# Two layers of graph attention on one core: a second-last superchunk's sums in three parts, and indices doubled step by step

## The chip, the cores and the metric

The kernel runs on one core of a Trainium2 chip. Its five engines work side by side, each through its own queue of instructions in order: PE (TensorE, matrix products), DVE (VectorE), ACT (ScalarE), POOL (GpSimd) and SP (SyncE, which here only issues transfers). They wait for each other through semaphores. The metric is the device time of one execution in microseconds; the lower, the better. Every kernel is run several times, and the median is told.

## The reference

A layer norm and a relu, then two layers of graph attention (GAT) over 6250 nodes with 256 features and 200,000 edges that are sorted by their destination, then a residual. Cut to what matters:

```python
def _add_self_loops(src, dst, ea, n):
    cnt = segment_sum(ones, dst)
    loop = segment_sum(ea, dst) / maximum(cnt, 1.0)[:, None]
    return concat([src, idx]), concat([dst, idx]), concat([ea, loop])

def _gat(x, src, dst, ea, Wg, a_s, a_d, Wge, a_e, b, n, h, f):
    hx = (x @ Wg).reshape(n, h, f)
    he = (ea @ Wge).reshape(-1, h, f)
    al = leaky_relu(einsum(hx, a_s)[src] + einsum(hx, a_d)[dst] + einsum(he, a_e), 0.2)
    al = exp(al - segment_max(al, dst)[dst])
    al = al / segment_sum(al, dst)[dst]
    return segment_sum(hx[src] * al[:, :, None], dst).reshape(n, h * f) + b

h = maximum(layernorm(x), 0.0)
te = relu(edge_attr @ We0 + be0) * exp(h @ Wo0 + bo0)[src][:, None]
h1 = relu(_gat(h, *_add_self_loops(src, dst, te), 4 heads of 64) + h)
te = relu(edge_attr @ We1 + be1) * exp(h1 @ Wo1 + bo1)[src][:, None]
h2 = _gat(h1, *_add_self_loops(src, dst, te), 1 head of 256) + h1
out = x + h2 + h
```

So each edge fetches the transformed row of its source, scales it by a softmax weight over the edges of the same destination, and the rows are added up by destination. Layer 1 needs all rows that layer 0 has made.

## The kernel before

**Steps.** The 200,000 edges are 1563 chunks of 128. Chunks are grouped into 66 superchunks a layer: 64 of 24 chunks, then one of 14 and one of 13. One step handles one superchunk of one layer; 132 steps in all, each with a dictionary (`st` for the step at hand, `nx` for the next, `pv` for the one before, `late` for the one before that, `after` for the first step of the next layer). In a superchunk each of the 128 partitions holds a run of C neighbouring edges.

**What a step does.** `gather(st)` issues one indirect DMA for each chunk from POOL's queue; it fetches 128 rows of a table in HBM (`self.T[l]`, seen as `self.rows[l]`) into the tile G, by the indices in `self.src[:, o:o+C]`, and between two of them POOL writes a small tile, `gap` (L799, L803). There are three buffers of G. The rows of layer 1's table are twice as long as those that are gathered, so its indices are the sources times two; L750 doubles them, all 1563 columns in one DVE instruction, while layer 0 ends.

`logits` (DVE) computes the attention logits and two scans along the partition's edges, which give maxima by destination within the partition. `ends` has PE transpose the scans' last columns into the PSUM tile `lf`; `links` (DVE) scans these across partitions, from the state that the superchunk before left, and has PE transpose the result back. `maxima` (DVE, ACT) ends with the exponentials in `k_w`. `scale` (DVE) multiplies the gathered rows by them, `carried` (DVE) adds in row 0 what the superchunk before leaves for a destination that both have. `onehots` builds S, a matrix for each chunk that says which edge belongs to which destination, and `sums` (PE) adds up the products S x G of all chunks in one PSUM tile, u. `evict` (ACT) copies it to the SBUF tile U.

`spread`, `parts`, `blocks`, `rphase1`, `rphase2`, `adst` and `edge_rows` prepare for the next step what depends on the edge attributes and on the destinations (`rphase1` yields in the middle, and uses PE and ACT).

**Finish and rows.** `finish` is `nodes0` or `nodes1`. Both begin with `merge`, small DVE instructions and an ACT exponential that join the self loop to the sums; in layer 0 follow an ACT relu `hw` (marked by `st["hw"]`) and six elementwise instructions of 256 columns, which an argument can put on POOL instead of DVE; in layer 1 two DVE instructions make the output rows `o`. In layer 0, `rows1` transposes the new rows on PE with a copy on ACT, `rows2` multiplies them by the next layer's weights into the PSUM tile `fin` (there is one), and `rows3` adds the bias (DVE, L434), takes an exponential (ACT) and writes the rows to `self.T[1]` by a DMA of SP's queue. In layer 1 `rows1` and `rows2` do nothing and `rows3` writes `o` to the output: by SP's queue for the first 64 superchunks, and for the last two by an indirect DMA of POOL's queue, whose index tile two DVE instructions make at that place (L1247, L1248). Writes to the same tensor at addresses known only at run time wait for each other.

**The last two superchunks of a layer** are handled together by `ending`, once for layer 0 (then `after` is layer 1's first step) and once for layer 1 (then `after` is None). In it `st` is the superchunk of 14 chunks, `nx` that of 13. The order of the calls is the order in every engine's queue: nothing is scheduled anew. After layer 0, `gather(after)` can start only when all of `self.T[1]` has been written. `ending` gives `finish` of `pv` and of `st` to POOL (`Z`). `sums(nx, first=1)` starts with chunk 1 and takes chunk 0, which `carried` changes, last.

Of the kernel before, what the change touches and what calls it, by code (L numbers as in the profile page):

```python
# [22 lines left out]
F32 = mybir.dt.float32  # L23
BF = mybir.dt.bfloat16
I32 = mybir.dt.int32
AF = mybir.ActivationFunctionType
OP = mybir.AluOpType
# [4 lines left out]
P = 128  # L32
C = 24
# [46 lines left out]
class Kernel:  # L80
# [480 lines left out]
    def index_group(self, g, pool, di):  # L561
# [23 lines left out]
        for pen, e in zip((self.fpen, self.lpen), ends):  # L585
            t = pool.tile([P, 4 * C], F32, name="gt", bufs=2)
            e3 = e.to_broadcast([P, n, c])
            V.tensor_sub(v3(t[:, :w]), *((d3, e3) if pen is self.fpen else (e3, d3)))
            yield
            V.tensor_scalar(pen[:, o:o + w], t[:, :w], 1.0, -BIG, op0=OP.min, op1=OP.mult)  # L590
            yield
# [117 lines left out]
    def ending(self, st, nx, pv, late, after):  # L709

        nc, k = self.nc, st["k"]
        Z = nc.gpsimd
        self.load_lb(k + 3)
        self.gather(nx)
        drain(self.logits(st))
        self.ends(st)
        self.spread(nx)
        self.parts(nx)
        y = self.rphase1(nx)
        next(y)  # L720
        self.links(st)
        if late:
            self.rows2(late)
        self.blocks(nx)
        drain(y)
        self.load_ea(k + 2)
        self.rphase2(nx)
        self.adst(nx)
        drain(self.maxima(st))
        drain(self.scale(st))  # L730
        self.carried(st)
        self.sums(st)
        self.edge_rows(nx)
        drain(self.logits(nx))
        self.ends(nx)
        self.onehots(nx)
        if late:
            self.rows3(late)
        if pv:
            drain(self.finish(pv, Z))  # L740
        self.links(nx)
        self.load_fl(k + 2)
        drain(self.maxima(nx))
        self.evict(st)
        y = self.rphase1(after) if after else iter(())
        next(y, None)
        c = nx["C"]
        drain(self.scale(nx, cuts=(1, 1 + c // 2, c)))
        if after:
            nc.vector.tensor_scalar(self.src, self.src, 2.0, None, op0=OP.mult)  # L750
        drain(self.scale(nx, cuts=(0, 1)))
        self.carried(nx)
        self.sums(nx, first=1)
        self.evict(nx)
        drain(self.finish(st, Z))
        if pv:
            self.rows1(pv)
            self.rows2(pv)
            self.rows3(pv)
        drain(y)  # L760
        f = self.finish(nx)
        while after and "hw" not in nx:
            next(f)
        self.rows1(st)
        self.rows2(st)
        drain(f)
        self.rows3(st)
        self.rows1(nx)
        self.rows2(nx)
        self.rows3(nx)  # L770
        if after:
            self.gather(after)
            self.nodes(after)
            self.spread(after)
            self.parts(after)
            self.blocks(after)
            self.rphase2(after)
            self.adst(after)
            self.edge_rows(after)
            self.onehots(after)  # L780
# [224 lines left out]

    def ends(self, st):


        e = st["ends"]
        self.nc.tensor.transpose(self.lf[0:e.shape[1], 1:P + 1], e, self.ident)  # L1010
# [85 lines left out]
                                    .to_broadcast([P, c1 - c0, H, L.F]), op=OP.mult)  # L1096
            yield

    def sums(self, st, first=0):
        nc, L, c = self.nc, st["L"], st["C"]  # L1100
        G, S = st["G"], st["S"]
        st["u"] = self.ps_1.tile([P, 512], F32, name="u")
        for j in range(c):
            i = (j + first) % c
            nc.tensor.matmul(st["u"][:, :L.W], S[:, i, :], G[:, i, 0:L.W], start=(j == 0), stop=(j == c - 1))  # L1105

    def evict(self, st):
        L = st["L"]
# [125 lines left out]
    def rows3(self, st):  # L1234
        nc, L, s = self.nc, st["L"], st["s"]
        if L.l == 0:
            self.table_row(st)
            r = self.row(0, s)
            nc.sync.dma_start(self.T[1][ds(r, M), :], st["trow"][1:M + 1, :])
            return  # L1240
        o, out = st["o"], self.a["out"]
        if s < self.direct:
            r = self.row(1, s)
            nc.sync.dma_start(out[ds(r, M), :], o[1:M + 1, :])
        else:
            idx = self.np_.tile([P, 1], I32, name="oidx")
            nc.vector.tensor_add(idx, self.base_f[:, s:s + 1], self.iota_m)  # L1247
            nc.vector.memset(idx[0:1, :], 1 << 20)  # L1248
            nc.gpsimd.indirect_dma_start(  # L1249
                out=out[:, :], out_offset=bass.IndirectOffsetOnAxis(ap=idx[:, 0:1], axis=0), in_=o,  # L1250
                in_offset=None, bounds_check=self.N - 1, oob_is_err=False)
# [119 lines left out]
def drain(g):  # L1371
    for _ in g:
        pass
# [93 lines left out]
```

## Time and profile before

| | us |
|---|---|
| median of 3 runs | 4556.36 |
| lowest and highest of them | 4551.79, 4559.2 |
| the profiled execution | 4555.93 |
| its span, from the first instruction to the last | 4554.1 |
| POOL busy | 3915.8 (86%) |
| PE busy | 3065.9 (67%) |
| DVE busy | 2901.8 (64%) |
| ACT busy | 516.8 (11%) |

The profile comes from one execution. Its page gives busy time by engine and groups of instructions; a row of a group has the line, engine, operation, output and inputs, the count, the busy time, the mean of one in ns, the idle time of the engine before them, and which other work ended that idle time. Rows in order of time have the start and the duration in us, then the instruction, and in brackets the engine's idle time before it and what ended it. Where a row says "issue", the engine waited for nothing that the profile shows. Several like instructions in a row can be merged (x2, x28). PEld are PE's weight loads. fp32 products go through PE in two passes, so the sums of 14 chunks show as x28.

### The profile page before, as it was taken

The numbers are of one execution on the slowest core, as the hardware profiler recorded it, in microseconds if no ns is written. First come the engines' busy times: TensorE is split into PE (matmuls) and PEld (weight loads), VectorE is DVE, ScalarE is ACT, GpSimd is POOL, SyncE is SP. The second block draws the span as 40 slices with busy tenths as digits, with TensorE's granted clock in tenths as the row PEclk, the third lists the DMA queues.
The fourth block names the chain that finished last, engine by engine and source line by source line (L and its number), as shares of the span: only waits on it lengthen the run. The fifth ranks groups of instructions, "written<-read, shape, count | busy, mean of one in ns | idle before, by whom it ended". The sixth has DMA issues, their size and how long they took to land. (4 is left out here: it accounts for less than half of the span.)

```text
span 4554.1 us, 37613 instructions
## 1 busy us (share of the span) xinstructions
PE 3065.9 (67%) x9916; PEld 1899.5 (42%) x9916; DVE 2901.8 (64%) x6675; ACT 516.8 (11%) x1150; POOL 3915.8 (86%) x6365
## 2 busy tenths in 40 slices
PE   8777677667677677677746566666666665666665
PEld 6444444444444344444424334333343343433433
DVE  7877667677677677676745555555554555555655
ACT  5111111111111111111100000000000000000000
POOL 6888888888888888888878888888888888888885
PEclk9877777777777777777767777777777777777777
DMA  6444444444444444444434444444444444444442
GB/s 224 130 136 134 126 129 136 124 127 136 125 128 135 125 128 135 125 130 134 119 98 124 116 128 122 118 128 128 111 128 121 124 123 128 122 116 122 128 116 74
DMA packets 231112, 576.39 MB, mean 127 GB/s; under 512 B 63097, under 2 KB 87871, under 8 KB 230825
## 3 DMA queue, kind: packets, MB, share of 16 engines
q0 software_dynamic: 150144, 422.75, 35.2%
q1 hardware_dynamic: 80331, 150.52, 10.0%
q8 instruction: 79, 1.29, 0.1%
q14 instruction: 142, 1.16, 0.1%
q10 hardware_dynamic: 416, 0.67, 0.1%
HBM read 542.72 MB, written 31.09 MB: 126 GB/s over the span
## 5 line engine op out<-in xcount | busy, mean ns | idle before, releaser
L799 POOL DMA_INDIRECT G<-T,src x3102 | 2969.6, 957 | 553.1 <-issue 518.7
L1105 PE MATMUL u<-G,S 128*128 128x270 f32 (+1 forms) x6252 | 1461.0, 393 | 106.7 <-DVE G L1085 97.6
L1105 PEld LDWEIGHTS u<-G,S 128*128 128x128 f32 x6252 | 1189.5, 192 | 388.0 <-DVE G L1085 162.1
L803 POOL MEMSET gap<- 128x208 f32 x3102 | 893.3, 288 | 1.8
L1095 DVE TENSOR_TENSOR G<-G,kps 128x6144 f32<-128x6144 f32 (+3 forms) x136 | 853.0, 6274 | 0.0
L885 PE MATMUL y<-ea,webd 64*128 64x384 f32 (+1 forms) x1056 | 749.7, 860 | 67.3 <-ACT R L890 66.7
L1010 PE MATMUL lf<-ident,fb 128*36 128x128 f32 (+1 forms) x132 | 53.3, 404 | 1093.3 <-DVE fb L1002 772.3
L987 DVE TENSOR_TENSOR G<-rt,G 128x96 f32<-128x96 f32 (+1 forms) x132 | 30.2, 228 | 1138.9 <-DMA G<-T,src 1138.6
L1010 PEld LDWEIGHTS lf<-ident,fb 128*36 128x36 f32 (+1 forms) x132 | 15.7, 119 | 1134.6 <-DVE fb L1002 819.2
L899 PE MATMUL zad<-R,wea 128*64 128x384 f32 (+1 forms) x1056 | 476.0, 815 | 0.5 <-DVE aq L952 0.3
L890 ACT ACTIVATE R<-y,webd 128x768 f32<-128x768 f32 x260 | 233.2, 897 | 2015.2 <-PE lf L1027 1647.7
L930 DVE TENSOR_TENSOR S<-kps,loc 128x3072 f32<-128x3072 f32 x132 | 437.5, 3315 | 4.5
L885 PEld LDWEIGHTS y<-ea,webd 64*128 64x128 f32 x1056 | 300.9, 314 | 311.8 <-issue 192.5
L899 PEld LDWEIGHTS zad<-R,wea 128*64 128x64 f32 x1056 | 160.7, 207 | 319.0 <-issue 214.0
L945 PE MATMUL zad<-a,Q 128*128 128x12 bf16 (+1 forms) x132 | 24.9, 188 | 174.6 <-DVE a L943 174.6
L430 PE MATMUL fin<-wg,h1T 128*128 128x260 f32 x264 | 135.3, 667 | 2.3 <-ACT h1T L1200 2.3
L973 DVE STREAM_TRANSPOSE rt<-zad 128x768 f32<-128x768 f32 (+1 forms) x130 | 124.9, 960 | 12.1 <-PE zad L959 11.2
L914 DVE TENSOR_TENSOR lb<-lb,kps 128x1536 bf16<-128x1536 bf16 (+1 forms) x68 | 112.7, 1658 | 0.0
L1110 ACT ACTIVATE U<-u 128x270 f32<-128x270 f32 (+1 forms) x132 | 51.9, 393 | 493.7 <-PE u L1105 493.7
L1041 DVE SCALAR_TENSOR_TENSOR m<-fpen,lf,m 128x24 f32<-128x24 bf16 (+1 forms) x66 | 16.4, 249 | 132.8 <-PE lf L1027 132.6
L945 PEld LDWEIGHTS <-Q 128*128 128x128 bf16 x132 | 13.7, 104 | 208.3 <-DVE a L943 198.6
L430 PEld LDWEIGHTS fin<-wg,h1T 128*128 128x128 f32 x264 | 75.6, 316 | 52.1 <-issue 36.6
(201 smaller groups left out, 2287.5 us busy)
## 6 DMA issues: line engine op xcount, KB each, us to landing
G<-T,src POOLq DMA_INDIRECT x3102, 2.8
ea<-in_ea_dram SPq DMA_DIRECT2D x64, 768.0 KB
lb<-locrow SPq DMA_DIRECT2D x64, 384.0 KB
T<-t1row SPq DMA_DIRECT2D x66, 227.5 KB
tw<-T SPq DMA_DIRECT2D x66, 225.8 KB
tw<-T SPq DMA_DIRECT2D x66, 117.2 KB
tw<-in_x_dram SPq DMA_DIRECT2D x66, 112.0 KB
out_dram<-fb SPq DMA_DIRECT2D x64, 112.0 KB
```

The lines of the kernel that those rows point to most:

```text
L430: self.nc.tensor.matmul(ps[:, :L.MW], hT[:, k, :], self.wg[L.l][:, k, :], start=(k == 0), stop=(k == 1))
L799: nc.gpsimd.indirect_dma_start(out=G[:, c, 0:L.TW], out_offset=None, in_=self.rows[L.l][0:n * (1 + L.l), :], in_offset=bass.IndirectOffset ...
L803: nc.gpsimd.memset(self.gap, 0.0)
L885: nc.tensor.matmul(y[:, o], self.webd[l][r, :], ea[r, w], start=True, stop=True)
L890: nc.scalar.activation(R[:, i, :32 * c].rearrange("p (b n) -> p b n", b=2), y.rearrange("p (b n) -> p b n", b=2)[:, :, :16 * c], AF.Relu, ...
L899: nc.tensor.matmul(st["zad"][i * PH:(i + 1) * PH, o], self.wea[l][0], R[:, i, w], start=True, stop=False)
L914: V.tensor_tensor(lb[:, :, :n], lb[:, :, :n], self.k_part.unsqueeze(2).to_broadcast([P, i, n]), op=OP.is_equal)
L930: nc.vector.tensor_tensor(st["S"][:, c0:c1, :], self.k_iota.unsqueeze(1).to_broadcast(w), self.loc[:, o + c0:o + c1].unsqueeze(2).to_broad ...
L973: V.transpose(rv[:, :32 * c].rearrange("p (b n) -> p b n", b=2), z.rearrange("p (b n) -> p b n", b=2)[:, :, :16 * c])
L1010: self.nc.tensor.transpose(self.lf[0:e.shape[1], 1:P + 1], e, self.ident)
L1095: nc.vector.tensor_tensor(v, v, pw[:, c0:c1, :].unsqueeze(3) .to_broadcast([P, c1 - c0, H, L.F]), op=OP.mult)
L1105: nc.tensor.matmul(st["u"][:, :L.W], S[:, i, :], G[:, i, 0:L.W], start=(j == 0), stop=(j == c - 1))
```

## The change

In `ending`, the sums of `st` are no longer issued in one piece. `sums` takes ranges of chunks and can be called several times for one step: the first third, then the logits and `ends` of `nx`, the second third, then the one-hots and links of `nx`, and the last third. `sums(nx, (1, c), (0, 1))` is the order of before (chunk 0 last). The finish of `pv` and its place before the links, and the row of `late`, move behind the sums of `nx`; finish never uses POOL any more. The finish of `st` comes before the eviction of `nx`, wholly in layer 1, and up to its `hw` in layer 0. In layer 1 the rows of `pv` and `st` are written as soon as their finish is issued; in layer 0 the row of `pv` follows the finish of `st`, and the row of `st` stands inside the finish of `nx`, behind its `hw`.

The index tiles of the two indirect writes are made at the start of `ending`. And `src` is doubled in `ends` of each step of layer 0, for that step's columns, behind the logits that have waited for their gather; the doubling of all columns is gone.

```diff
     def ending(self, st, nx, pv, late, after):
         nc, k = self.nc, st["k"]
-        Z = nc.gpsimd
         self.load_lb(k + 3)
         self.gather(nx)
+        for q in () if after else (st, nx):
+            q["idx"] = idx = self.np_.tile([P, 1], I32, name="oidx")
+            nc.vector.tensor_add(idx, self.base_f[:, q["s"]:q["s"] + 1], self.iota_m)
+            nc.vector.memset(idx[0:1, :], 1 << 20)
         drain(self.logits(st))
         self.ends(st)
...
         self.carried(st)
-        self.sums(st)
+        c, h = nx["C"], st["C"] // 3
+        self.sums(st, (0, h))
         self.edge_rows(nx)
         drain(self.logits(nx))
         self.ends(nx)
+        self.sums(st, (h, 2 * h))
         self.onehots(nx)
-        if late:
-            self.rows3(late)
-        if pv:
-            drain(self.finish(pv, Z))
         self.links(nx)
+        self.sums(st, (2 * h, st["C"]))
         self.load_fl(k + 2)
         drain(self.maxima(nx))
         self.evict(st)
         y = self.rphase1(after) if after else iter(())
         next(y, None)
-        c = nx["C"]
         drain(self.scale(nx, cuts=(1, 1 + c // 2, c)))
-        if after:
-            nc.vector.tensor_scalar(self.src, self.src, 2.0, None, op0=OP.mult)
         drain(self.scale(nx, cuts=(0, 1)))
         self.carried(nx)
-        self.sums(nx, first=1)
-        self.evict(nx)
-        drain(self.finish(st, Z))
+        self.sums(nx, (1, c), (0, 1))
+        if late:
+            self.rows3(late)
         if pv:
+            drain(self.finish(pv))
             self.rows1(pv)
             self.rows2(pv)
+            if not after:
+                self.rows3(pv)
+        f = self.finish(st)
+        while after and "hw" not in st:
+            next(f)
+        if not after:
+            drain(f)
+            self.rows3(st)
+        self.evict(nx)
+        drain(f)
+        if after and pv:
             self.rows3(pv)
         drain(y)
+        self.rows1(st)
+        self.rows2(st)
         f = self.finish(nx)
         while after and "hw" not in nx:
             next(f)
-        self.rows1(st)
-        self.rows2(st)
+        if after:
+            self.rows3(st)
         drain(f)
-        self.rows3(st)
         self.rows1(nx)
         self.rows2(nx)
         self.rows3(nx)
...
     def ends(self, st):
+        if st["L"].l == 0:
+            src = self.src[:, st["o"]:st["o"] + st["C"]]
+            self.nc.vector.tensor_scalar(src, src, 2.0, None, op0=OP.mult)
         e = st["ends"]
...
-    def sums(self, st, first=0):
+    def sums(self, st, *parts):
         nc, L, c = self.nc, st["L"], st["C"]
         G, S = st["G"], st["S"]
-        st["u"] = self.ps_1.tile([P, 512], F32, name="u")
-        for j in range(c):
-            i = (j + first) % c
-            nc.tensor.matmul(st["u"][:, :L.W], S[:, i, :], G[:, i, 0:L.W], start=(j == 0), stop=(j == c - 1))
+        for a, b in parts or ((0, c),):
+            for i in range(a, b):
+                j = st["n"] = st.get("n", -1) + 1
+                if j == 0:
+                    st["u"] = self.ps_1.tile([P, 512], F32, name="u")
+                nc.tensor.matmul(st["u"][:, :L.W], S[:, i, :], G[:, i, 0:L.W], start=(j == 0), stop=(j == c - 1))
...
     def rows3(self, st):
...
-            idx = self.np_.tile([P, 1], I32, name="oidx")
-            nc.vector.tensor_add(idx, self.base_f[:, s:s + 1], self.iota_m)
-            nc.vector.memset(idx[0:1, :], 1 << 20)
+            idx = st["idx"]
             nc.gpsimd.indirect_dma_start(
```

## The prediction

> **What bounds the kernel now.** I read the page first, then the groups of POOL, then the two stretches in which POOL issues no gathers, then those stretches instruction by instruction.
>
> ```profile
> span 4554.1 us, 37613 instructions
> ...
> PE 3065.9 (67%) x9916; PEld 1899.5 (42%) x9916; DVE 2901.8 (64%) x6675; ACT 516.8 (11%) x1150; POOL 3915.8 (86%) x6365
> ...
> L799 POOL DMA_INDIRECT G<-T,src x3102 | 2969.6, 957 | 553.1 <-issue 518.7
> ```
>
> POOL is the busiest engine, and of the 553.1 us that it idles before gathers, 518.7 are its own issuing: almost nothing holds it up. The next rows are stretches: length, then busy time and count of PE, PE's weight loads, DVE, ACT and POOL, then the granted clock, and DMA. The first pair is the long runs of the two layers, the second the stretch between the last gather of layer 0 and the first of layer 1 ("the turn"), and that from the last gather to the end ("the end").
>
> ```profile
> 266.00:2232.00 1966.00, 1399.20 (x4350) 851.64 (x4350) 1399.90 (x3292) 242.39 (x567) 1732.40 (x2785) 0.74 0.47 129
> 2345.10:4477.00 2131.90, 1352.47 (x4347) 828.56 (x4347) 1178.30 (x2381) 168.51 (x314) 1877.01 (x3025) 0.73 0.45 122
> ...
> 2268.10:2309.75 41.65, 25.82 (x82) 17.62 (x83) 28.75 (x87) 6.83 (x19) 10.01 (x16) 0.78 0.11 38
> 4512.74:4554.10 41.36, 15.49 (x55) 11.99 (x54) 16.56 (x58) 1.66 (x6) 2.31 (x4) 0.71 0.04 11
> ```
>
> A gather and its memset are two POOL instructions, so a gather comes every 1966/1392.5 = 1.412 us in layer 0 and 2131.9/1512.5 = 1.409 us in layer 1. The time is set by this pace, by the start, and by the two stretches of some 41.5 us in which the pace is broken. The change touches the two stretches, and puts one small DVE instruction into each of the 66 steps of layer 0.
>
> **The doublings in layer 0.** 66 instructions (128x24 int32, the last two 128x14 and 128x13) replace one of 128x1563.
>
> ```profile
> L987 DVE TENSOR_TENSOR G<-rt,G 128x96 f32<-128x96 f32 x63 | 16.2, 257 | 357.1 <-DMA G<-T,src 356.8
> ...
> L1127 DVE TENSOR_SCALAR mw<-U,cnt 128x4 f32<-128x4 f32 x62 | 22.6, 364 | 0.0
> ...
> L1124 DVE TENSOR_SCALAR cnt<-U 128x1 f32<-128x1 f32 x62 | 8.3, 134 | 0.0
> ...
> 162.62 0.95 POOL L799 DMA_INDIRECT G<-T,src  x1 [5.81 <-ACT U L1110]
> ```
>
> No row has this shape. The nearest tensor_scalar rows bound it at 0.13 and 0.36 us. The one of 1563 elements took 0.96 (below), 0.6 ns an element, so 24 add next to nothing to a fixed cost; I take 0.2, nearer to the row with the least. It stands in DVE's queue behind the logits, so that the gather whose indices it overwrites has landed, and ahead of Q, the parts, the links and all that follows. DVE waits 356.8/63 = 5.7 us a step for the gather, so 0.2 us disappears in that wait. Without that cover it would cost 66 x 0.2 = 13 us. The cover is missing in the first steps, where POOL waits once, 5.81 us, for step 0's sums to be evicted: there it costs 0.2 us (0.13 to 0.36).
>
> A second price is possible, that it slows POOL. The two layers give a bound: by these stretches a step of 24 gathers has 3292/58 = 57 DVE instructions in layer 0 and 2381/63 = 38 in layer 1, 19 fewer, and its gathers are 2.3 ns further apart, 0.055 us a step. If one more instruction did all of that, it would be 3.6 us; a nineteenth of it is 0.2 us. I take 0.2 and keep 0 to 3.6.
>
> The Trainium skill speaks against this: "SBUF — State Buffer", section "Who interferes with whom", says that a tensor_scalar in a 2-port mode and GpSimd, which writes gather descriptors, exclude each other, the second to come being fully blocked. By it POOL could lose each doubling's whole length. The L1127 row, a tensor_scalar that averages 364 ns, suggests that here it is DVE that comes second.
>
> **The turn.** Rows by engine: DVE, then PE, ACT and POOL.
>
> ```profile
> 2250.93 0.14 DVE L1121 TENSOR_SCALAR cnt<-U 128x1 f32<-128x1 f32 x1
> ...
> 2253.40 0.42 DVE L1178 TENSOR_TENSOR fa<-tw,mw 128x256 f32<-128x256 f32 x1
> ...
> 2255.78 0.17 DVE L575 CAST gf<-gi 128x26 f32<-128x26 int32 x1
> ...
> 2262.66 0.21 DVE L1037 TENSOR_TENSOR m<-fb 128x56 f32<-128x56 f32 x1
> ...
> 2265.77 0.26 DVE L1064 COPY G<-kps 128x56 f32<-128x56 f32 x1 [1.26 <-ACT kps L1060]
> ...
> 2271.75 0.21 DVE L987 TENSOR_TENSOR G<-rt,G 128x52 f32<-128x52 f32 x1
> ...
> 2275.14 0.42 DVE L434 TENSOR_TENSOR t1row<-fin,bias 128x260 f32<-128x260 f32 x1
> ...
> 2279.29 0.47 DVE L1020 TENSOR_TENSOR_SCAN cl<-fl,cl,lf 4x129 f32<-4x129 f32 x1 [1.38 <-PE lf L1010]
> ...
> 2280.22 0.51 DVE L1037 TENSOR_TENSOR m<-fb 128x52 f32<-128x52 f32 x1
> ...
> 2283.60 3.41 DVE L1095 TENSOR_TENSOR G<-G,kps 128x1536 f32<-128x1536 f32 x2
> 2286.93 0.96 DVE L750 TENSOR_SCALAR src<-src 128x1563 int32<-128x1563 int32 x1
> ...
> 2289.13 0.13 DVE L1121 TENSOR_SCALAR cnt<-U 128x1 f32<-128x1 f32 x1
> ...
> 2299.70 0.43 DVE L1178 TENSOR_TENSOR fa<-tw,mw 128x256 f32<-128x256 f32 x1
> ...
> 2299.22 2.10 PE L430 MATMUL fin<-wg,h1T 128*128 128x260 f32 x4 [0.65 <-ACT h1T L1200]
> ...
> 2302.71 0.66 PE L1198 MATMUL fin<-ident,fb 128*128 128x128 f32 x2 [1.39 <-DVE t1row L434]
> ...
> 2297.07 0.90 ACT L890 ACTIVATE R<-y,webd 128x768 f32<-128x768 f32 x1 [0.82 <-PE y L885]
> ...
> 2301.35 0.42 ACT L1184 ACTIVATE fb<-fb 128x256 f32<-128x256 f32 x1 [2.18 <-DVE fb L1182]
> ...
> 2309.75 1.06 POOL L799 DMA_INDIRECT G<-T,src  x1 [10.18 <-DMA T<-t1row]
> ```
>
> Before, the links of the last superchunk start at 2279.29, held by the transpose L1010, which stands behind all 14 matmul groups of the second-last. Afterwards that transpose stands behind four. DVE then runs: logits and one-hots 2275.14 - 2271.75 = 3.39, a doubling 0.2, so links at 2275.3; links 0.93; maxima and exponential 2265.77 - 1.26 - 2262.66 + 0.3 = 2.15 (the 3.38 from 2280.22 to 2283.60 fell together with POOL's share of finish, which is gone); scale starts at 2278.4, not 2283.60. Scale and carry: 2289.13 - 2283.60 less the 0.88 of the doubling = 4.65, to 2283.0.
>
> Now DVE must pay for what POOL did. It runs the late row (0.35) and all of finish for pv, 2255.78 - 2250.93 = 4.85, to 2288.2; the first half of st's finish, 2253.40 - 2250.93 = 2.47, and its elementwise half, 2.38, to 2293.1; pv's row, 0.35; and nx's first half, 2.47, to 2295.9. In front of nx's elementwise half now stands st's row, which waits for st's table matmuls: their input passes transposes (0.66) and, on ACT, a copy that stands behind the second half of R (0.90), some 1.8 us from 2293.4, and then the matmuls take 2.10 us, or half of that at full clock, so the row ends at 2296.5 to 2297.4. From nx's elementwise half to the first gather the trace has 2309.75 - 2299.70 = 10.05, of which 0.94 (2301.35 + 0.42 to 2302.71) was the transposes' wait for st's row, now past: 9.1. The gather comes at 2305.6 to 2306.5. I take 2306.2: **3.5 us** gained. Queued behind DVE's waits here are only finish and row work, all on this chain. The four table writes keep their order on SP, each after the one before it has landed: the late one moves from behind the one-hots to 2283.6; pv's, at 2293.8, has over 4 us until nx's elementwise half (2297 to 2299) writes the same row tile again; st's, at 2297.5, has 5 us until nx's goes at some 2303. POOL's queue loses 14 instructions, and nothing stands in it ahead of the gather.
>
> **The end.** There finish never used POOL, so DVE's work is the same in another order; the rows are DVE, PE, one stretch of all engines, POOL.
>
> ```profile
> 4514.86 0.18 DVE L987 TENSOR_TENSOR G<-rt,G 128x13 f32<-128x13 f32 x1 [3.06 <-DMA G<-T,src]
> ...
> 4515.90 0.15 DVE L927 COPY kps<-lastloc 128x1 f32<-128x1 f32 x1
> ...
> 4517.89 0.21 DVE L1126 SCALAR_TENSOR_TENSOR mg<-U,cnt,tw 128x1 f32<-128x1 f32 x1
> ...
> 4520.74 0.47 DVE L1020 TENSOR_TENSOR_SCAN cl<-fl,cl,lf 1x129 f32<-1x129 f32 x1
> ...
> 4523.21 3.74 DVE L1095 TENSOR_TENSOR G<-G,kps 128x1536 f32<-128x1536 f32 x3
> ...
> 4527.59 0.20 DVE L1126 SCALAR_TENSOR_TENSOR mg<-U,cnt,tw 128x1 f32<-128x1 f32 x1
> ...
> 4511.04 7.82 PE L1105 MATMUL u<-G,S 128*128 128x261 f32 x28 [3.83 <-DVE G L1085]
> ...
> 4525.05 8.88 PE L1105 MATMUL u<-G,S 128*128 128x261 f32 x26 [3.12 <-issue]
> ...
> 4511.00:4514.00 3.00, 2.96 (x7) 2.36 (x8) 0.77 (x3) 0.00 (x0) 1.86 (x4) 0.52 0.37 101
> ...
> 4539.61 1.02 POOL L1249 DMA_INDIRECT out_dram<-fb,oidx  x1 [26.59 <-DVE flagf L789]
> 4544.64 1.01 POOL L1249 DMA_INDIRECT out_dram<-fb,oidx  x1 [4.00 <-DVEq L1259]
> ```
>
> Data land at 4514.86 as before. pv's finish (4520.74 - 4517.89 = 2.85) leaves its place in front of the links, so these start at 4517.9, scale at 4520.4, and scale with carry ends at 4524.7 (4527.59 less 2.85). Then come pv's and st's finish, 2 x 2.85, to 4530.4, while PE still sums. st's write is issued at 4530.5 instead of 4539.61. The second write keeps its distance, 4544.64 - 4539.61 = 5.03: not before 4535.6. Is nx ready by then? A group took 7.82/14 = 0.56 or 8.88/13 = 0.68 us. Four groups end at 4513.3, PE waits for the logits until 4515.9, four more end at 4518.5, the link's transpose at 4519.1, the last six at 4522.4; after an eviction the 13 of nx, at 0.68, end at 4531.8, and eviction and finish at 4535.2. So the second write is at 4535.6, **9.0 us** earlier. The index tiles, 4 DVE instructions, move from behind the last finish to the front, under the wait for the gather.
>
> **Sum.** -9.0 - 3.5 + 0.2 + 0.2 = -12.1 us. The profiled execution took 4555.93 with a span of 4554.1, and is 0.43 below the median; so 4543.8 there, and 4556.36 - 12.1 = **4544 us** at the median.
>
> **Rivals.** (1) PE stays at half clock through the parts, because its work is cut up: a group then takes 0.91 (the stretch to 4514 shows a clock of 0.52, so the 7.82 us hold 2.9 at half clock and 4.9 at full, which makes 0.46 a group at full), the ten later groups end at 4525.3 and the carry waits 1.6 us for them; at the turn the same costs 1.9: 4547.5. For: PE pauses 2.6 us at 4513.3. Against: the half clock of the 4511.04 row followed a pause of 3.83 us, a longer one, and was over 2.9 us later. The Trainium skill ("TensorE: Matmul & The Clock Gate", Part 1) has the clock fall after an idle window of about 3.4 us, which would spare this pause.
> (2) The turn gains nothing: eviction of nx now stands on ACT behind pv's transposed copy and st's exponential, and st's row holds DVE. The end alone: 4556.36 - 9.0 + 0.4 = 4547.8.
> (3) Slower: each doubling stops POOL for its whole length. At 0.36 us, 66 x 0.36 = 23.8, less 12.5: 4567.7; it decides from 12.5/66 = 0.19 us a step. For: 364 ns of L1127 beside 134 of L1124, two tensor_scalars of almost the same small size, show that DVE and POOL do get in each other's way. Against: the layers' nearly equal pace. The Trainium skill's rule, above, is this rival.
> (4) The end's writes stay a chain of three: pv's write goes out on SP at 4527.6, in the middle of the stretch, and st's must wait for it as nx's does for st's. At the same 5.03 us the writes go at 4532.6 and 4537.7 and the end gains 7.0: 4546.4. For: all write the same tensor. Against: the 5.03 holds 1.02 of POOL's own issue, which SP's does not.
>
> **How the numbers follow.** Forecast 0.63, rivals (1) 0.12, (2) 0.12, (3) 0.06, (4) 0.07. A difference of 0.2%, 9.1 us, is what a measurement of this kernel can tell. The forecast with its own spread (turn 1 to 4.5, end 7 to 9.5) is faster in nine of ten, (1) and (2) lie just inside the bound and count a third as faster, (4) just outside and counts two thirds, (3) is slower in two of three. So faster 0.57 + 0.08 + 0.05 = 0.70, slower 0.04, the rest the same. The range runs from 4539 (turn 4.5, end 9.5 and some 3 us of spread, as the runs of before have around their median) to 4554 (rivals (1), (2) and (4) with the same spread and the doublings' 3.6).
>
> **What would show it.** Layer 0's gather distance stays 1.412 us; the stretch between the layers' gathers is about 38 us, the last stretch 32; st's write falls under the last sums, the writes are 5.0 us apart. Wrong if the distance in layer 0 grows by over 5 ns, if DVE idles over 2 us ahead of st's row, or if nx's sums end after 4532.

## The result, and the profile after

The changed kernel takes 4546.49 us (median of 20 runs, 4544.47 to 4549.57); the kernel before, on the same chip, 4555.09 (20 runs). The ratio is 0.9981, with a 95% interval of 0.9974 to 0.9988: 8.6 us less. The prediction was 12.1 less, 4544.

The profiled execution, from the page and from the view by stretches (length, busy time of PE, weight loads, DVE, ACT and POOL, granted clock, DMA): layer 0, turn, end.

```profile
span 4543.4 us, 37664 instructions
...
PE 3051.1 (67%) x9916; PEld 1889.7 (42%) x9916; DVE 2914.5 (64%) x6752; ACT 517.3 (11%) x1152; POOL 3908.8 (86%) x6351
```

```profile
266.00:2232.00 1966.00, 1388.59 (x4350) 846.05 (x4350) 1409.75 (x3346) 242.26 (x567) 1732.83 (x2782) 0.74 0.48 129
2268.15:2306.65 38.50, 24.67 (x82) 16.24 (x83) 29.93 (x99) 7.79 (x21) 0.29 (x2) 0.81 0.12 43
4510.01:4543.40 33.39, 14.85 (x54) 10.66 (x53) 16.25 (x54) 1.74 (x6) 2.32 (x4) 0.70 0.06 14
```

POOL's finish work has left the turn (16 instructions before, 2 now), and DVE has 99 there instead of 87. The four gathers that bound the pieces of the span, in order of time:

```profile
160.47 0.95 POOL L811 DMA_INDIRECT G<-T,src  x1 [4.69 <-ACT U L1127]
...
2267.20 0.95 POOL L811 DMA_INDIRECT G<-T,src  x1 [0.17 <-issue]
...
2306.65 0.95 POOL L811 DMA_INDIRECT G<-T,src  x1 [38.21 <-DMA T<-t1row]
...
4509.06 0.95 POOL L811 DMA_INDIRECT G<-T,src  x1 [0.17 <-issue]
```

With the same four gathers of before (162.62, 2267.16, 2309.75, 4511.79), this is where the 10.7 us between the two spans lie:

| piece | before | after | difference | predicted |
|---|---|---|---|---|
| start, to POOL's restart behind step 0's sums | 162.62 | 160.47 | -2.15 | +0.2 |
| layer 0, to its last gather | 2104.54 | 2106.73 | +2.19 | +0.2 |
| turn, to layer 1's first gather | 42.59 | 39.45 | -3.14 | -3.5 |
| layer 1, to its last gather | 2202.04 | 2202.41 | +0.37 | 0 |
| end, to the end of the span | 42.31 | 34.34 | -7.97 | -9.0 |

The start is chance: POOL restarted between 159.34 and 162.44 in the profiles of the changed kernel and of four kernels below whose code up to there is the same (one_sum, pv_first, short_second, late_write). Without it 8.55 remain, the 8.6 of the medians.

The turn, DVE and PE:

```profile
2270.85 3.44 PE L1122 MATMUL u<-G,S 128*128 128x270 f32 x8 [4.24 <-DVE G L1100]
2274.30 2.25 PE L1122 MATMUL u<-G,S 128*128 128x270 f32 x8
2275.25 0.46 DVE L1035 TENSOR_TENSOR_SCAN cl<-fl,cl,lf 4x129 f32<-4x129 f32 x1
2276.78 0.21 DVE L1059 TENSOR_TENSOR mt<-fpen,lf 128x52 f32<-128x52 bf16 x1 [0.40 <-PE lf L1042]
2278.69 3.74 DVE L1110 TENSOR_TENSOR G<-G,kps 128x1536 f32<-128x1536 f32 x3
2281.09 6.19 PE L1122 MATMUL u<-G,S 128*128 128x270 f32 x26
2283.34 0.41 DVE L434 TENSOR_TENSOR t1row<-fin,bias 128x260 f32<-128x260 f32 x1
2297.18 0.43 DVE L434 TENSOR_TENSOR t1row<-fin,bias 128x260 f32<-128x260 f32 x1 [1.01 <-PE fin L430]
2302.93 0.43 DVE L434 TENSOR_TENSOR t1row<-fin,bias 128x260 f32<-128x260 f32 x1 [2.96 <-PE fin L430]
```

The links start at 2275.25 (predicted 2275.3), the scale at 2278.69 (2278.4), the late row at 2283.34 (2283.0). The row of the second-last holds DVE for 1.01 us.

The end:

```profile
4507.90 3.85 PE L1122 MATMUL u<-G,S 128*128 128x261 f32 x8 [3.90 <-DVE G L1100]
4512.14 0.18 DVE L999 TENSOR_TENSOR G<-rt,G 128x13 f32<-128x13 f32 x1 [3.47 <-DMA G<-T,src]
4513.32 0.42 PE L1025 MATMUL lf<-ident,fb 128*33 128x128 f32 x1 [1.57 <-DVE fb L1014]
4513.53 3.69 PE L1122 MATMUL u<-G,S 128*128 128x261 f32 x8
4517.51 0.24 DVE L1056 SCALAR_TENSOR_TENSOR m<-fpen,lf,m 128x13 f32<-128x13 bf16 x1 [1.25 <-PE lf L1042]
4520.78 5.99 PE L1122 MATMUL u<-G,S 128*128 128x261 f32 x26 [0.48 <-ACT U L1127]
4529.18 1.02 POOL L1264 DMA_INDIRECT out_dram<-fb,oidx  x1 [18.88 <-DVE mw L1144]
4532.35 1.00 POOL L1264 DMA_INDIRECT out_dram<-fb,oidx  x1 [2.14 <-DVE flag_i L802]
```

The second part of the sums takes 0.92 us a group, and the second link transpose stands behind it: DVE waits 1.25 us. The longest wait of before is gone. In it, DVE stood in st's finish until ACT had evicted nx's sums and then taken the exponential; now st's finish comes ahead of that eviction. The same instruction, before and after:

```profile
4534.57 0.22 DVE L1137 SCALAR_TENSOR_TENSOR mg<-U,mw 128x1 f32<-128x1 f32 x1 [6.14 <-ACT mw L1135]
```

```profile
4527.18 0.22 DVE L1154 SCALAR_TENSOR_TENSOR mg<-U,mw 128x1 f32<-128x1 f32 x1 [0.36 <-ACT mw L1152]
```

The two writes are 3.17 us apart; before, 5.03. Behind the second write there were 4554.1 - 4544.64 = 9.46 us before; now 11.05. The queues' own instructions at the writes and at the last branch, of before and of after (line, queue, operation; least, median and most duration in ns, first and last start), and the landing of the second write, tell why:

```profile
L1249 POOLq EVENT_SEMAPHORE  x4: 43/43/4424, 4522.7 to 4539.5; - x4
L1259 POOLq EVENT_SEMAPHORE  x4: 17/43/43, 4545.5 to 4547.4; - x4
L1259 POOLq INC_SWDGE_SEM  x1: 1268/1268/1268, 4547.5 to 4547.5; - x1
DMA to landing us min/median/max: 2.7/2.7/2.7
```

```profile
L1264 POOLq EVENT_SEMAPHORE  x4: 43/43/2569, 4527.9 to 4529.0; - x4
L1274 DVEq EVENT_SEMAPHORE  x1: 21/21/21, 4536.6 to 4536.6; - x1
L1274 POOLq EVENT_SEMAPHORE  x4: 17/43/43, 4533.2 to 4536.7; - x4
L1274 POOLq INC_SWDGE_SEM  x1: 1268/1268/1268, 4536.8 to 4536.8; - x1
DMA to landing us min/median/max: 4.3/4.3/4.3
```

Before the second write POOL waits on a semaphore for the first one's landing: 4.42 us before (4539.5 to 4543.9; by the updates of its semaphore in the trace the first write landed 4.23 us after its start), 2.57 now (to 4531.6; it landed after 2.38), which is over before the data of the second are ready. Behind the second write POOL's INC_SWDGE_SEM follows that write's own landing, at 4544.64 + 2.7 and at 4532.35 + 4.3, and in both the span ends 6.6 us behind the start of INC_SWDGE_SEM. So what grew by 1.6 us is the landing. The slow write is each time the one in flight when the engines take the kernel's last branch (from 4540.4 before, from 4532.6 now): before the first, now the second. In all fourteen profiles of this case the write in flight there landed after 4.0 to 4.6 us and the other after 2.4 to 2.8. That it is the branch, and how, no run shows. POOL does not wait for DVE there, though DVE goes on at almost the same time (4536.6): in late_write, below, POOL's INC_SWDGE_SEM starts at 4538.5 and DVE goes on at 4538.7.

### The profile page after: what moved, and what is told of

Read it like the earlier page. It is cut to its first block, busy times and chain, and to the rows that moved or that the text cites. A ratio compares the mean times of both kernels' runs of the same rounds, so it can differ in the third digit from the quotient of the medians.

```text
span 4543.4 us, 37664 instructions
## 1 busy us (share of the span) xinstructions
PE 3051.1 (67%) x9916; PEld 1889.7 (42%) x9916; DVE 2914.5 (64%) x6752; ACT 517.3 (11%) x1152; POOL 3908.8 (86%) x6351
## 3 DMA queue, kind: packets, MB, share of 16 engines
q1 hardware_dynamic: 80331, 150.52, 10.1%
## 5 line engine op out<-in xcount | busy, mean ns | idle before, releaser
L985 DVE STREAM_TRANSPOSE rt<-zad 128x768 f32<-128x768 f32 (+1 forms) x130 | 124.9, 961 | 11.2 <-PE zad L971 10.3
```

Source lines behind the costliest of these rows:

```text
L985: V.transpose(rv[:, :32 * c].rearrange("p (b n) -> p b n", b=2), z.rearrange("p (b n) -> p b n", b=2)[:, :, :16 * c])
```

## The experiments

Each piece is measured as above, in one profiled execution. The first eight ran on two chips where the kernel before took 4555.70 and 4555.78 us.

**What the doublings cost.** One doubling of all 1563 columns back at the turn (turn_double); the doublings in the steps, in the kernel before (double_only); seven more in-place multiplications by 1.0 a step (double_x8); the same seven writing spare PSUM (psum_x8).

```diff
 # turn_double: none in ends(), and in ending()
+        if after:
+            nc.vector.tensor_scalar(self.src, self.src, 2.0, None, op0=OP.mult)
 # double_x8, in ends()
+            for _ in range(7):
+                self.nc.vector.tensor_scalar(src, src, 1.0, None, op0=OP.mult)
 # psum_x8: the same with out=self.kps[:, 400:400 + st["C"]]
```

> The changed kernel with the doublings of the steps taken out and the one doubling of all 1563 columns put back at the turn. From POOL's restart after step 0's sums to layer 0's last gather the trace took 2104.5 us before and 2106.7 after the change. Theory 1, the 66 doublings slow POOL: this distance falls back to 2104.5, the turn's stretch grows from 39.4 by up to 0.9 (the doubling stands ahead of the carry and so of all finishes), and the time lies 1.3 us below the changed kernel, ratio to the kernel before 0.9978. Rival, the distance differs by chance and the doublings cost nothing: the distance stays within 0.5 of 2106.7 or wanders, and the time lies 0.9 us above the changed kernel, ratio 0.9983.

> The kernel before with the doublings moved into the 66 steps, and nothing else changed. Theory 1: restart to last gather in layer 0 is 2106.7 us, not 2104.5, and the turn's stretch stays at 41.5 to 42.6, since there the one doubling stood under PE's sums; ratio to the kernel before 1.0003 to 1.0005. Rival: distance 2104.5, ratio 1.0000.

> The changed kernel with seven more instructions of the doubling's shape (times 1.0, in place) behind each of the 66 doublings. DVE has 5.7 us of wait a step to hide them in. Theory 1 with 33 ns a doubling: 66 x 7 x 0.033 = 15 us more in layer 0, restart to last gather 2122, ratio to before 1.0014. If each stops POOL for its whole length of 0.25 us: 116 us more, ratio 1.024. Rival, no price: distance 2106.7, ratio 0.9981 to 0.9986 (the first steps have no wait to hide the seven in, 1 to 2 us).

> As the run with eight doublings a step, but the seven more write a spare stretch of PSUM instead of overwriting the indices in SBUF. If a doubling's price comes from DVE's two-sided use of SBUF, this one costs POOL nothing: restart to last gather 2106.7, ratio 0.9981 to 0.9986. If it comes from DVE's time, or from overwriting the indices near POOL's reads, at least the first of these two gives the same as the run with eight doublings (2122).

| kernel | median us | ratio, 95% interval | layer 0 | turn | end |
|---|---|---|---|---|---|
| turn_double | 4545.97 | 0.9979 [0.9970, 0.9988] | 2104.93 | 41.42 | 33.97 |
| double_only | 4557.53 | 1.0005 [0.9996, 1.0014] | 2106.51 | 42.94 | 41.93 |
| double_x8 | 4551.41 | 0.9992 [0.9983, 1.0001] | 2104.81 | 44.65 | 33.01 |
| psum_x8 | 4549.25 | 0.9987 [0.9977, 0.9996] | 2104.42 | 45.98 | 33.43 |

One doubling a step costs layer 0 about 2 us, in the old order and in the new; eight cost it nothing, where I had expected 2106.7 at the least. So doublings don't stop POOL. They do get in each other's way, but DVE pays. The lines of the added instructions in double_x8 and psum_x8 (ns, least, median, most):

```profile
L1024 DVE TENSOR_SCALAR src<-src x462: 173/281/397, 137.3 to 2279.8; 128x24 int32<-128x24 int32 x150, 128x14 int32<-128x14 int32 x2, 128x13 int32<-128x13 int32 x2
```

```profile
L1025 DVE TENSOR_SCALAR kps<-src x462: 174/186/188, 136.8 to 2279.8; 128x24 f32<-128x24 int32 x150, 128x14 f32<-128x14 int32 x2, 128x13 f32<-128x13 int32 x2
```

From SBUF to SBUF an instruction takes up to 397 ns; writing PSUM it takes 188 at most. The Trainium skill ("SBUF — State Buffer", section "Who interferes with whom") has a tensor_scalar in a 2-port mode and GpSimd shut each other out, the later one waiting; the spread agrees with it, with DVE as the later one.

The 2 us come from position, as far as the traces show it. One step of the turn_double run, then of the changed kernel, near the start of the scale:

```profile
1086.76 0.30 DVE L1075 TENSOR_TENSOR G<-m,isl 128x96 f32<-128x96 f32 x1
1087.09 0.95 POOL L813 DMA_INDIRECT G<-T,src  x1 [0.17 <-issue]
```

```profile
1087.95 1.08 POOL L811 DMA_INDIRECT G<-T,src  x1 [0.17 <-issue]
1087.96 0.30 DVE L1076 TENSOR_TENSOR G<-m,isl 128x96 f32<-128x96 f32 x1
```

A doubling shifts what DVE does later in the step against the gathers. G<-m,isl, which ended just ahead of a gather, now starts beneath one, and that gather takes 1.08 us instead of 0.95. In the changed kernel the gather at this place, one of a step's 24, is lengthened in 27 steps, in the kernel before in none; over all gathers what is above 0.95 us adds up to 12.3 us in layer 0, against 9.7. In turn_double it is 10.1; with eight doublings, in double_x8, 13 gathers at this place are lengthened, but only 77 in all, against 100 in the changed kernel and 84 before, and the sum is 10.2. On these chips the six profiles with one doubling a step have 2106.5 to 2108.1 us for layer 0, the four others 2104.4 to 2104.9. That it is G<-m,isl and no neighbour was not tried.

In the stretches the added instructions count: double_x8 lost 5.2 us at the turn. And turn_double lost 1.97 there, about as much as the 1.80 that layer 0 gave back. But only 0.97 of it is the doubling; the rest is DVE's wait for the second link transpose, 1.79 us for 0.40, with the second part of the sums partly at half clock (3.06 us for 2.25). So moving the doubling gained nothing, and may have cost some 0.8 us, which the two ratios, 0.9979 and 0.9981, can't tell.

**Parts and order, each alone.** one_sum sums the second-last in one piece at the first part's place; pv_first puts the late row and finish of pv back ahead of the links.

```diff
 # one_sum
+        self.sums(st)
-        self.sums(st, (0, h))
-        self.sums(st, (h, 2 * h))
-        self.sums(st, (2 * h, st["C"]))
 # pv_first; these lines no longer stand behind the sums of nx
         self.onehots(nx)
+        if late:
+            self.rows3(late)
+        if pv:
+            drain(self.finish(pv))
         self.links(nx)
```

> The sums of the second-last superchunk again in one piece, all 14 groups ahead of the last one's ends and links; the rest as in the changed kernel. Theory: the parts matter where the 14 groups hold up the link transpose for longer than DVE has other work. At the turn they start at 2270.85 and take 7.6 us, to 2278.5, so the links start at about 2279 instead of 2275.25: the turn goes from 39.45 to about 43. At the end they start at 4507.9 and take some 7.8 us, to 4515.7, so the links start at 4516.5 instead of 4515.17, but the wait of 1.25 us for the second transpose goes: the end stays within 0.5 us of 34.34. Together +3.3 us, 4549.8. Rival: the parts carry the whole gain at both places (turn 43, end 42): 4558. Rival: PE's half clock through the parts eats what they gain: 4546.5, no change.

> The late row and the whole finish of the superchunk before the last pair again stand ahead of the last one's links (on DVE in both layers), everything else as in the changed kernel. Theory: DVE is the engine that both stretches run on, and its work is the same in either order; what counts is that it doesn't wait. So the links come 2.9 us (end) and 5.2 us (turn) later, the waits for PE's second transpose (1.25 and 0.40 us) go, and the last sums end 1.6 us later at the end, some 0.2 us after DVE is free for them: end +0.2, turn +0 to 1; 4546.7 to 4548. Rival: the place of finish is the gain, since links, scale and last sums are the chain: end +2.85, turn +4.85, 4554.

| kernel | median us | ratio, 95% interval | turn | end |
|---|---|---|---|---|
| one_sum | 4552.74 | 0.9995 [0.9986, 1.0005] | 44.44 | 36.57 |
| pv_first | 4552.91 | 0.9995 [0.9985, 1.0005] | 43.94 | 36.16 |

Both cost more than I had expected; pv_first comes nearer to its rival. Either half alone makes the turn longer than before (42.59), and only both together shorten it. I put that down to finish, which has gone from POOL to DVE; no run puts it back. At the end either half alone is enough for most of the gain: 36.57 and 36.16 are 5.7 and 6.2 us below the 42.31 of before, with 2.2 and 1.8 more for the two together. What these kernels share there, above all st's finish ahead of the eviction of nx (DVE's wait of 6.14 us is 0.37 in both), no run takes out alone. In one_sum DVE waits 5.20 us at the turn for the link transpose behind 14 groups. In pv_first it waits later; PE, ACT and DVE:

```profile
2287.85 6.19 PE L1123 MATMUL u<-G,S 128*128 128x270 f32 x26
2293.88 0.38 PE L1216 MATMUL fin<-ident,fb 128*128 128x128 f32 x2
2294.30 0.38 ACT L1218 ACTIVATE h1T<-fin 128x256 f32<-128x256 f32 x1 [5.44 <-PE fin L1216]
2294.58 0.20 ACT L1165 ACTIVATE mw<-mw 128x8 f32<-128x8 f32 x1
2294.81 0.16 DVE L1167 TENSOR_TENSOR mg<-U,mw 128x4 f32<-128x4 f32 x1 [4.93 <-ACT mw L1165]
```

The last sums start 6.5 us later against the last gather than in the changed kernel, pv's transposes stand behind them on PE, ACT's copy waits for those, and the exponential of st's finish stands behind that copy: DVE idles 4.93 us for a queue it does not share. My theory that DVE's work in another order costs the same left this out.

**PE's clock, and the writes.** short_second gives the second part 2 groups and the third 8; late_write moves only the call of the second-last's write behind the last finish.

```diff
 # short_second
+        g = h + h // 2
-        self.sums(st, (h, 2 * h))
+        self.sums(st, (h, g))
-        self.sums(st, (2 * h, st["C"]))
+        self.sums(st, (g, st["C"]))
 # late_write
         if not after:
             drain(f)
-            self.rows3(st)
         self.evict(nx)
...
         drain(f)
+        if not after:
+            self.rows3(st)
         self.rows1(nx)
```

> The second part of the sums has 2 groups instead of 4, the third 8 instead of 6. Theory: in the profiled run PE worked through the second part at half clock (0.92 us a group), and the second link transpose stood behind it, so that DVE waited 1.25 us at the end and 0.40 at the turn. With 2 groups less ahead of it, that transpose comes 1.85 us earlier at half clock and 0.9 at full: both waits go, end 33.1 and turn 39.1, 4545.0. If what is moved behind (2 groups) then holds up the last sums, nothing is gained: 4546.5. Rival: the wait isn't PE's but that of the scan and its semaphore; then the wait stays at 1.25.

> In layer 1 the write of the second-last superchunk is issued behind the last one's finish, so that both last writes are ready at once (near 4531.8). Theory: the second write waits until the first has landed. Before, the two were 5.03 us apart with the first in the moment in which all engines took the last branch, in the changed kernel 3.17 with the first 2.5 us ahead of it. If falling together with the branches' fetch of instructions makes the first write slow to land, they are again about 5 us apart: first at 4532, second at 4537, end +4.5 less what hides. If 3.17 is the plain distance of two chained writes, the second goes at 4535.2, +2.8. If the writes aren't chained at all, and 3.17 was only the time of the last finish (2.87 and its semaphore), the second goes at 4533.2 and the end comes at most 1 us later.

short_second: 4546.85 us, ratio 0.9980 [0.9970, 0.9989]; turn 38.88, end 34.88. The wait for the second transpose is gone at the turn and 0.20 us at the end, as expected, but there the 16 matmuls behind it, nearly all at half clock, took 6.08 us, to 4521.72, and DVE waited 1.45 us for their eviction instead: nothing gained. late_write (one execution, 4546.94) left the two writes where they were, 3.17 us apart, as POOL's queue holds nothing between them; it is a repeat of the changed kernel, with one difference that no code explains. Its end, against the 4512.14 to 4517.51 above:

```profile
4510.82 3.45 PE L1123 MATMUL u<-G,S 128*128 128x261 f32 x8 [3.83 <-DVE G L1101]
4516.14 0.30 PE L1026 MATMUL lf<-ident,fb 128*33 128x128 f32 x1 [1.87 <-DVE fb L1015]
4516.28 1.93 PE L1123 MATMUL u<-G,S 128*128 128x261 f32 x8
4518.94 0.25 PE L1043 MATMUL lf<-ident,cl 33*128 33x33 f32 x1 [0.74 <-DVE cl L1038]
```

Here the second part runs at full clock, 0.48 us a group, and DVE doesn't wait for the second transpose. From DVE's taking of the last data to the second write this run takes 19.13 us, double_x8 19.12, psum_x8 19.30, all with that part at full clock; turn_double 20.11 and the changed kernel 20.21, at half clock. So in these five executions the clock goes with about 1 us of the end.

**On a slower chip.** The last four kernels met chips on which the kernel before took 4742.81 us (three kernels) and 4692.81 (the last); only pieces that begin with the data in place compare with the runs above. swap_writes issues the last superchunk's write ahead of the second-last's; the rows that both cover then keep the other's value. double_by16 doubles in six instructions, after every sixteenth superchunk and for the last two. warm adds matmuls that nobody reads.

```diff
 # double_by16, in ends()
+        if st["L"].l == 0 and (s % 16 == 15 or s >= self.NS - 2):
+            lo = st["o"] - (15 * C if s < self.NS - 2 else 0)
 # warm, in ending(), ahead of sums(st, (0, h))
+        for _ in range(14):
+            nc.tensor.matmul(st["u"][:, 0:P], self.ident, self.ident, start=True, stop=True)
 # and in layer 1, ahead of ends(nx)
+            for _ in range(12):
+                nc.tensor.matmul(w[:, 0:P], self.ident, self.ident, start=True, stop=True)
```

> In layer 1 the last superchunk's write is issued first and the second-last's behind it, so both are ready when the first goes out, 23.0 us behind the last gather. The late_write run had moved only the call: POOL's queue holds nothing else there, and the writes stayed 3.17 us apart. Theory: the 3.17 is set by the data (the last finish takes 2.87 us, and its semaphore), the writes don't wait for each other, and the 5.03 of the kernel before came from the branch at the end; then the second goes at most 1.4 us behind the first and the end is at most 1.2 us later than 34.3. Rival: the second write waits until the first has landed: 3.2 us or more behind it, end 36 to 37.5. Rival: a write issued while the engines fetch what follows the branch takes 5 us: end 39.

> Layer 0's doublings in six instructions (four of 384 columns, after every sixteenth superchunk, and the last two's) instead of 66. Theory: the 2.2 us that layer 0 loses in the changed kernel are not the doublings' own time nor a fight with POOL for a port, since eight doublings a step cost POOL nothing (2104.81 us from the restart to the last gather, as 2104.54 before, against 2106.73 with one): one doubling shifts DVE's later instructions by 0.3 us against the gathers, so that G<-m,isl falls beneath the start of a gather and that one takes 1.08 us instead of 0.95. Without it in most steps the distance is 2104.9, and the time 4544.5. Rival: the six larger ones, which touch the same index tile that POOL reads, stop it for their length: 2106.5 or more, no gain.

> Adds matmuls of the identity by itself that nobody reads: 14 ahead of the second-last superchunk's sums in both endings, and in layer 1 also 12 between their first and second part, to keep PE's clock up. Theory: the end of the changed kernel depends on whether PE is granted its full clock for the parts: in runs with the second part at full clock the last stretch took 33.0 to 33.4 us, at half clock 34.0 to 34.9. With the clock kept, both parts take 1.9 us, DVE does not wait for the second link transpose, and the end is 33.1 in every execution; at the turn 0.4 to 1 us less. 4545.0. Rival: the clock falls all the same, and the added matmuls at half clock (0.45 us each) hold the parts up: end 35 to 37, 4548.

In swap_writes (one execution, 4729.97) both writes are ready at once, and the second waits for the first to land:

```profile
4714.15 1.03 POOL L1265 DMA_INDIRECT out_dram<-fb,oidx  x1 [34.15 <-DVE flag_i L803]
4718.52 1.00 POOL L1265 DMA_INDIRECT out_dram<-fb,oidx  x1 [3.34 <-DMA out_dram<-fb,oidx]
```

So the writes are chained, 4.37 us apart here: the rival, not the theory. The first write meets the branch and lands after 4.10 us, the second after 2.84, and the tail is 9.58 us again, as before the change. The 3.17 us of the changed kernel is the time of the last finish (2.87) and what follows it; the first write has landed by then.

double_by16: 4736.34, ratio 0.9981 [0.9965, 0.9997]. Layer 0 takes 2165.56 us, against 2168.43 in swap_writes and 2168.83 in warm, whose layer 0 is that of the changed kernel: 2.9 less, the theory's sign, and more than its 1.8. What gathers take above 0.95 us adds up to 10.3 us, against 13.8. But on this chip other gathers of a step are the lengthened ones, and few of them start with G<-m,isl, so the sum bears the theory out, but not the instruction; and in the last kernel below, with the same six doublings on another chip, the sum is 15.6. The ratio is that of the changed kernel, 0.9981. warm: 4733.93, 0.9988 [0.9972, 1.0004], unclear. At the turn it does what it should (both parts at 2.0 us; from the sums' start to layer 1's first gather 35.61 us against 36.33 in swap_writes). At the end both parts took 2.0 us too, but the second set of added matmuls overran: DVE waited 0.79 us for the link transpose behind them.

The last kernel joins double_by16 and warm (8 matmuls in the second set) and moves the turn's row:

```diff
         if after:
+            for _ in range(4):
+                next(f)
             self.rows3(st)
```

> Three of the tried edits in one: the doublings in six instructions, the unread identity matmuls that keep PE's clock up (14 ahead of the sums in both endings, 8 between the first two parts in layer 1), and at the turn the second-last's table row behind the first four elementwise instructions of the last one's finish, where DVE has waited 1.01 us for its table matmuls. By the profiled run of the changed kernel: layer 0 2104.9 from the restart to the last gather (-1.8), the turn 38.0 (-0.4 for the link transpose, -1.0 for the row), the end 33.2 (-1.1): 4542, and 0.997 of the kernel before. Rival: the clock stays chance, the row's wait only moves to the next wait for PE (2.96 us, for the last one's matmuls): layer 0's share alone, 4544.7.

4669.86 us against 4692.81: ratio 0.9955 [0.9941, 0.9968]. From the sums' start to layer 1's first gather the turn takes 34.21 us (35.80 in the changed kernel); the rows of the second-last and the last:

```profile
2376.86 0.42 DVE L434 TENSOR_TENSOR t1row<-fin,bias 128x260 f32<-128x260 f32 x1
...
2380.81 0.43 DVE L434 TENSOR_TENSOR t1row<-fin,bias 128x260 f32<-128x260 f32 x1 [2.67 <-PE fin L430]
```

The 1.01 us wait is gone and has not moved on. At the end nothing was gained: both parts took 1.93 us, but DVE waited 0.43 and 0.84 us for the transposes, and the data were taken 20.35 us ahead of the second write. It beats the kernel before; whether it beats the changed kernel was not measured on one chip, and its 0.45% is more than these pieces explain.

## Why the prediction came out as it did

**The mechanism held.** Links held by four groups instead of fourteen, finish beneath the sums, POOL out of the turn: each DVE time at the turn was met within 0.4 us, and one_sum and pv_first show that there the cut and the order are both needed. At the end each alone brings most of the gain; that the rest hangs on st's finish beneath the sums is argued from DVE's wait of 6.14 us, not tried alone.

**The end, -7.97 for -9.0.** Two terms of the sum were wrong, and both hold the same delay. "The second write keeps its distance, 4544.64 - 4539.61 = 5.03" is the step that failed: that distance was a write ready at once waiting for the other, which met the last branch and took 4.23 us to land; with the data 3 us apart and the first landing in 2.38, it is 3.17, 1.9 us better. The time behind the second write, which I took as fixed, grew by 1.59, as now the second meets the branch and lands in 4.3 us instead of 2.7. So 0.3 of the 1.9 us are left. And four of the ten later groups were at half clock: rival (1), expected at 1.6 us in the carry, cost 1.25, in DVE's wait for the second link transpose. Together -9.56 at the second write and -7.97 at the end. That st's write would fall under the last sums was wrong too: these ended at 4526.77, at 0.46 us a group where I had taken 0.68.

**The turn, -3.14 for -3.5.** DVE's waits of 0.40 and 1.01 us; the second-last's row ended at 2297.61, 0.2 past the times that I gave it.

**Layer 0, +2.19 for +0.2.** Inside the bound of 0 to 3.6, but not for the reason that gave it: position against the gathers, not a share in DVE's instructions. A gather still comes every 1966/1391 = 1.413 us.

**The rivals.** (1) came true in part, at the end. (2) fell, the turn gained. (3) fell with eight doublings a step, which left layer 0 at 2104.81 us. (4) fell: pv's write at 4526.07 did not hold up st's, which went when its data were ready. The Trainium skill ("TensorE: Matmul & The Clock Gate", Part 1), weighed there for the fall of the clock, also has the activity window run free of the kernel; the runs agree, as one code got 3.69 us and 1.93 for its second part.

## What to carry to other kernels

Cutting a block of matmuls so that a small transpose gets through pays only when the engine whose work it releases is not then held by a third queue: follow what stands behind each wait on PE, on ACT and on DVE together. A distance between two transfers is a price only while both are ready; ask what set it before keeping it in a sum. The time behind the last transfer is no constant: it holds that transfer's landing, and a delay that goes with an event, here the last branch, stays when another transfer takes its place there.

## What the hardware showed beyond that

PE's granted clock in two executions of the same order of work at the end, after and late_write, by stretches:

```profile
4507.50:4511.50 4.00, 3.60 (x8) 2.51 (x8) 1.13 (x5) 0.00 (x0) 2.48 (x4) 0.50 0.38 100
4513.00:4517.00 4.00, 3.68 (x9) 2.57 (x9) 3.18 (x7) 0.00 (x0) 0.00 (x0) 0.50 0.00 0
4517.50:4520.00 2.50, 2.50 (x12) 2.08 (x12) 2.20 (x7) 0.19 (x1) 0.00 (x0) 1.00 0.01 3
```

```profile
4516.00:4519.00 3.00, 2.12 (x10) 1.53 (x10) 2.92 (x7) 0.00 (x0) 0.00 (x0) 1.00 0.00 0
```

In the first, 3.85 us of work, a pause of 1.57 and 3.7 us more passed at half clock; in the second, the clock was 0.50 from 4511 to 4513 and 1.00 from 4514 on, so 3.45 us of work raised it, and a pause of 1.87 did not lower it. What raised the clock in one and not in the other no run here shows.

Past the branch at the kernel's end DVE took some 4.0 us to its next instruction (4540.5 to 4544.5 before, 4532.7 to 4536.6 after), ACT 0.4 (4540.4 to 4540.8, 4532.6 to 4533.0). An indirect write in flight there landed after 4.0 to 4.6 us, one that was not after 2.4 to 2.8, in fourteen profiles.
